# Cross-attention queries multiplied by blocks, and sums and loads moved to other steps, in a decoder with gated cross-attention

## The chip, the cores and the metric

The kernel runs on one core of a Trainium2 chip, in float32. The metric is device time in microseconds (us), the median of several runs. The engines are TensorE (PE, with its weight loads PEld), VectorE (DVE), ScalarE (ACT), GpSimd (POOL) and SyncE (SP), whose queue issues nearly all DMA transfers. Every engine works through its own instructions in the order of the program.

## The reference

Sixteen sequences of 128 tokens with 512 features go through a decoder layer (self-attention, cross-attention to an encoder context, MLP, each after a layer norm and added to the residual), and then through a gated cross-attention to the same context. Sixteen heads have 32 features each.

```python
ln_out = layernorm(hidden_states, ln1_s, ln1_b)
q, k, v = jnp.split(ln_out @ w_qkv + b_qkv, 3, axis=-1)
x = hidden_states + merge_heads(attention(split_heads(q), split_heads(k), split_heads(v), ltor_mask)) @ w_ao + b_ao
q = layernorm(x, ln2_s, ln2_b) @ w_q + b_q
k, v = jnp.split(encoder_states @ w_kv + b_kv, 2, axis=-1)
x = x + merge_heads(attention(split_heads(q), split_heads(k), split_heads(v), cross_mask)) @ w_co + b_co
x = x + gelu(layernorm(x, ln3_s, ln3_b) @ w1 + b1) @ w2 + b2
# gated: Q = x Wq', K and V from layernorm(context), a boolean mask
x = x + jnp.tanh(gate) * (out @ Wo.T)
```
`attention` multiplies the scores by the mask, subtracts 10000 (1 - mask), and takes a softmax over the keys.

## The kernel before

**Sections.** The 16 sequences are four groups of four batches. Each attention of a group is a section: A0 to A3 (self), B0 to B3 (cross), then the MLP over all groups, then D0 to D3 (gated). A section has 16 steps, four per batch. PE begins a batch in step 0, 4, 8 or 12 with its scores (into four "sc" PSUM banks), applies an older batch's probabilities to the values in steps 2, 6, 10, 14 (`mix`, the av matmuls), and makes its output projection (mo) two steps later. The work of a unit (four heads of a batch) moves down one step at a time: DVE scales the scores out of PSUM (`scale_unit`), POOL adds the mask term (`add_mask`); a step later DVE takes the minimum and ACT four exponentials with their sums (`exp_unit`); then DVE takes reciprocals and POOL normalizes (`norm_unit`); then DVE transposes within 32x32 squares and SP sends the unit to DRAM, from where pairs of units come back transposed (`receive_pair`).

**Beside a section.** While a section is attended, its steps also carry the projections of the next section (`jobs`) and the normalization and transposition of the tokens of the one after that (`prepare`): the queries, keys and values of B0 are made beside A3, those of B1 beside B0, of B2 beside B1, of B3 beside B2; beside B3 stand the start of the MLP and the first gated keys and values, beside D0 the projections of D1. `plan` collects lists of jobs with their steps, written out by hand. In each step the order is: receive, scores, what was put off by `afterwards` (DVE's first, then ACT's), the jobs, an older output projection, mix, prepare, transpose, normalize and exponentials, scale, mask (`attend`, lines 657 to 701).

**Blocks.** Most projections are done with seven quarter products instead of eight (`block_product`, lines 383 to 424): the operands are cut in 2x2 blocks, four sums of the weight's blocks (`left_blocks`) and four of the tokens' (`right_blocks`, in part in place) are made first, and products 1 to 7, of four matmuls 128x256 each, are added up. Products 1, 6 and 7 pile up in one PSUM bank ("mm0") and ACT copies it out after each, at once; 5 and 3 use "mm1" and 2 and 4 one of the two banks "pt", which the mix and the output projection use too; DVE adds these in the next step. Product 1 needs no sum; 6 needs the third weight sum and the second token sum, 7 the first and the third, 5 the second and the first, 3 the fourth weight sum, 4 the fourth token sum. `BLOCKS` (line 464) holds the steps of a self-attention section's three products, `CROSS_BLOCKS` (line 480) those of the cross keys and values. The cross queries are made in four chunks of four matmuls 128x512, in "mm0" and "mm1", copied out by ACT (`query_chunk`, line 921).

**Buffers.** Weights and weight sums lie in a pool of six buffers "w"; masks and some sums in two buffers "mask"; scores in seven "s"; parts received and gated tokens in three "pT". The token sums of a cross section's keys and values lie in the residual x of the group, which is put away in DRAM meanwhile (`keep_part`, `tokens_again`).

Of the kernel before, what the change touches and what calls it, by code (L numbers as in the profile page):

```python
# [16 lines left out]
P = 128  # L17
NB = 16
S = 128
Q = 32  # L20
# [32 lines left out]
def decoder_then_gated_cross_attention(ctx: ExitStack, tc: tile.TileContext, a: dict, out: bass.AP):  # L53
# [406 lines left out]
    def by_quarters(t):  # L460
# [17 lines left out]
    )  # L478

    CROSS_BLOCKS = (  # L480
        {6: (1,), 7: (6, 2), 9: (7, 5), 10: (4,), 11: (3,)},
        {11: (1,), 13: (6, 2), 14: (7, 5), 15: (4, 3)},
    )
    GATED_BLOCKS = (
# [156 lines left out]
    def attend(sections, ready, others, after=None):  # L641

        if not ready:
            sections[0].start(sections[1])
        at_start[0] = False
        units, batches = [], []  # L650
        projected = deque()

        def by_transfer(n):

            return min(n, (len(sections) * GB - 1) * GB) if ready else n

        def step(k, bt=None, jobs=(), ahead=None):

            m = k % GB
            pair = k - 5  # L660
            if pair % 2 and 0 <= pair < by_transfer(len(units)):
                receive_pair(*units[pair])
            if m == 0 and bt is not None:
                scores(bt)
            due()
            for job in jobs:
                job()
            if projected and (m == 0 or ready and bt is None):
                before = projected.popleft()
                if before.sec.deferred:  # L670
                    afterwards("act", lambda: before.sec.put_away(before))
                else:
                    out_project(before)
            done = k // GB - 2
            if ready and k == by_transfer(k) + 7:
                done = len(batches) - 1
                mix(batches[done])
                projected.append(batches[done])
            elif m == 2 and 0 <= done < len(batches) - ready:
                mix(batches[done])  # L680
                projected.append(batches[done])
            if ahead is not None:
                ahead.prepare(k % NS)
            if 0 <= k - 3 < len(units):
                (turn_unit if k - 3 < by_transfer(k) else turn_by_array)(*units[k - 3])
            def norm():
                if 0 <= k - 2 < len(units):
                    norm_unit(*units[k - 2])

            def exp():  # L690
                if 0 <= k - 1 < len(units):
                    least_unit(*units[k - 1])
                    exp_unit(*units[k - 1])


            for do in (exp, norm) if ready else (norm, exp):
                do()
            if bt is not None:
                for j in SCALED[m]:
                    scale_unit(bt, j)  # L700
                bt.sec.add_mask(by_head(bt.s[m]), bt.b)

        k = 0
        for i, sec in enumerate(sections):
            last = i + 1 == len(sections)
            jobs = others() if last else sections[i + 1].jobs()
            ahead = sections[i + 2] if i + 2 < len(sections) else after if i + 2 == len(sections) else None
            for b in range(GB):
                bt = Batch(sec, b)
                batches.append(bt)  # L710
                for m in range(GB):
                    units.append((bt, m))
                    step(k, bt, jobs.get(k % NS, ()), ahead)
                    k += 1
        while projected or k < len(units) + 2 * GB:
            step(k, jobs=jobs.get(k - len(units) + NS, ()))
            k += 1
# [14 lines left out]
    class SelfAttention(Section):  # L732
# [19 lines left out]
        def begin(self, following):  # L752
# [24 lines left out]
            for o in SelfAttention.weight_sums[0]:  # L777
                nc.gpsimd.tensor_tensor(*o)
            following.prepare(0)
            transposed_out(self.lnT, tp, "ln1_s", "ln1_b")  # L780

        def start(self, following):

            self.begin(following)
            _, todo = self.tiles()
            for o in todo:
                nc.vector.tensor_tensor(*o)
            key_sums, value_sums = self.weight_sums[1:]
            prepare = [lambda p=p: following.prepare(p) for p in (2, 4, 6, 9, 12, 13)], [0, 1, 2, 4, 6, 6]
            jobs = plan(  # L790
                *blocks_plan(self.products(), FIRST_BLOCKS), prepare,
                ([lambda o=o: nc.gpsimd.tensor_tensor(*o) for o in key_sums], [0, 1, 2, 3]),
                ([lambda o=o: nc.gpsimd.tensor_tensor(*o) for o in value_sums], [4, 5, 6, 6]),
                ([load_small, lambda: mask_terms(ms1, ma1)], [2, 5]),
                ([lambda b=b: load_batch(2, b) for b in range(2)], [3, 5]),
            )
            for p in range(max(jobs) + 1):
                due()
                for job in jobs[p]:
                    job()  # L800
            due()
# [18 lines left out]
        def jobs(self):  # L820
# [3 lines left out]
            if g > 1:  # L824
# [3 lines left out]
            return plan(  # L828
                *blocks_plan(first.products()[2:], FIRST_BLOCKS), (sums, [2, 3, 4, 5]),
                *blocks_plan(self.products(), SECOND_BLOCKS), *small_jobs(),  # L830
                ([lambda p=p: self.prepare(p) for p in (14, 15)], [0, 0]),
                ([lambda b=b: add_row(0, bo_row, b) for b in range(GB)], range(8, 12)),
                *gated_weight("k", act_tile("gw_k", "enc"), range(4, 12), range(9, 16, 2)),
            )
# [23 lines left out]

    def late_weights():

        return [lambda key=key, k=k: load_cross(key, k) for key in ("ck", "cv", "co") for k in range(KC)], range(12)

    class CrossAttention(Section):
        w_o = property(lambda self: w["co"])
# [32 lines left out]

        def jobs(self):
            g, n, lnT, encT = self.g, self.name, self.lnT, self.encT
            mask = work.tile([P, 2, GB, S], F32, tag="mask", name=f"mask_{g}", bufs=2)  # L900
# [4 lines left out]
            qkv_tiles(self)  # L905
            tokens_at = [x[g][:, b].rearrange("p (o t) -> p o t", t=HF) for b in range(3)]
            token_sides, sums = right_blocks(encT, tokens_at)
            if g == 0:
                self.begin()
            products = [  # L910
                block_product(halves(self.k), self.k_sides, token_sides, False, f"k_{n}", ("b_k", 0)),
                block_product(by_quarters(self.v), self.v_sides, token_sides, True, f"v_{n}"),
            ]
            return plan(
                ([lambda c=c: self.query_chunk(c) for c in range(KC)], [1, 2, 3, 5]),
                *blocks_plan(products, CROSS_BLOCKS), ([lambda: mask_terms(self.ms, self.ma)], [7]),
                ([lambda o=o: nc.gpsimd.tensor_tensor(*o) for o in sums], [0, 1, 2, 3]),
                *(self.weights_begin() if g == 0 else decoder[NG + g - 1].tokens_again([5, 9, 13])),
            )

        def query_chunk(self, c):
            project_chunk(self.q, w["cq"], self.lnT, c, f"q_{self.name}", "b_q", 0, ("mm0", "mm1")[c % 2])

        v_bias = "b_cv", 0

# [1 line left out]
            return [([lambda b=b: fetch_part(f"x_{self.name}", x[self.g], b) for b in order], at_)]  # L927

        def begin(self):
            t = wpool.tile([P, GB, 2, HF], F32, tag="w", name="sums_c")  # L930
            row = work.tile([P, 2, HF], F32, tag="row", name="sums_c_row", bufs=2)
            CrossAttention.sums_at = [t[:, n] for n in range(GB)] + [row, sums_c]
            CrossAttention.k_sides, CrossAttention.v_sides = [], []

        def weights_begin(self):

# [12 lines left out]
            def v_sum(n):  # L949
# [2 lines left out]
                todo["v"][n]()  # L952

            return (
                late_weights(), ([lambda n=n: k_sum(n) for n in range(4)], [4, 4, 5, 5]),
                ([lambda n=n: v_sum(n) for n in range(4)], [9, 10, 11, 12]),
            )

        def scale_mask(self, s, sc, b):
# [403 lines left out]
    class GatedAttention(Section):  # L1363
# [12 lines left out]
        def hidden_states(self, b, t=None):  # L1376
# [98 lines left out]
        def jobs(self):  # L1475
# [10 lines left out]
            by_dve, by_pool = (  # L1486
                lambda o, eng=eng: lambda: eng.tensor_tensor(*o) for eng in (nc.vector, nc.gpsimd)
            )
# [191 lines left out]
```

## Time and profile before

| | us |
|---|---|
| median of 3 runs (lowest, highest) | 1176.0 (1175.42, 1177.72) |
| profiled execution | 1175.37 |
| its span, first to last instruction | 1173.6 |
| A0 to A3, from scores to scores | 41.18, 103.13, 164.27, 225.41 to 288.33 |
| B0 to B3 begin at | 288.33, 350.06, 411.79, 474.79 |
| first gated scores | 950.89 |
| PE busy in the span | 1134.5 |

The profile's times are us from the span's start. A line of the order of time gives start, duration, engine, operation, the tile written and those read, the shape, how many were merged, and in brackets the idle time of the engine before it with what ended that. A line of a table by stretch gives, for every engine, its busy us and in brackets the number of instructions, then the granted clock of PE as a share of full speed, and DMA. All instructions have the same line number (L49, a helper's), so that one goes by tiles. The end of a section's last batches overlaps the next section's first.

### The profile page before, as it was taken

What the parts mean: (1) busy time and instruction counts of PE and PEld (TensorE: products, weight loads), DVE (VectorE), ACT (ScalarE), POOL (GpSimd) and SP (SyncE); (2) the same over time, 40 slices, a digit from 0 to 9 for tenths busy, and PEclk for the clock granted to TensorE, in tenths of its full rate; (3) what the DMA queues carried; (4) which work ended last, traced back from release to release, by engine and by line L of the source; (5) the groups of instructions that cost most, each with busy time, mean ns of one, the idle gap of its engine ahead of it and who ended that gap; (6) DMA issues with size and microseconds to landing.
All of it is one profiled execution on the core that took longest, in us unless ns stands there. A gap on an engine that the chain in (4) does not pass through costs nothing.

```text
span 1173.6 us, 21606 instructions
## 1 busy us (share of the span) xinstructions
PE 1134.5 (97%) x7202; PEld 864.2 (74%) x7202; DVE 766.9 (65%) x1513; ACT 608.4 (52%) x2129; POOL 698.0 (59%) x632
## 2 busy tenths in 40 slices
PE   6999999999999999998999999999999989999998
PEld 5877777657575747545788888888888767778775
DVE  7677878797878876865663633533432268878773
ACT  2467767666766766674221332232222238876763
POOL 6698878688868775684333423533441356554973
PEclk9999999999999999999999999999999999999999
DMA  6588968999888879998796686595467628888874
GB/s 217 150 219 226 234 191 216 252 235 252 212 230 203 243 208 242 253 285 260 249 291 225 195 263 200 193 310 207 153 204 249 188 61 230 227 233 238 243 208 160
DMA packets 325118, 259.75 MB, mean 221 GB/s; under 512 B 83528, under 2 KB 280336, under 8 KB 320144
## 3 DMA queue, kind: packets, MB, share of 16 engines
q1 hardware_dynamic: 324968, 258.38, 76.4%
q8 instruction: 57, 0.93, 0.3%
q14 instruction: 53, 0.43, 0.1%
q10 hardware_dynamic: 40, 0.01, 0.0%
HBM read 163.94 MB, written 94.37 MB: 220 GB/s over the span
## 4 chain that ended last, share of the span: by engine, by line
PE 49%; DMA 2%; DVE 2%; issue 1%; POOL 1%; ACT 1%; SPq 0%; DVEq 0%; POOLq 0%; ACTq 0%
PE o L49 16%; PE h L49 16%; PE mm_q_D L49 3%; PE mm_v_D L49 3%; PE mm_k_D L49 3%; PE mm_o_D L49 3%; PE sc_D L49 1%; PE av_D L49 1%; PE mo_D L49 1%; DMA away_B<-s_B 1%; PE mo_B L49 1%; SPq L49 0%; POOL x L49 0%; POOL s_B L49 0%; DVE s_D L49 0%
## 5 line engine op out<-in xcount | busy, mean ns | idle before, releaser
L49 DVE TENSOR_TENSOR h<-h,h 128x512 f32<-128x512 f32 x80 | 54.8, 686 | 112.8 <-PE h L49 112.5
L49 ACT ACTIVATE s_A<-s_A,mn_A 128x128 f32<-128x128 f32 x256 | 100.1, 395 | 50.9 <-issue 36.8
L49 ACT ACTIVATE s_B<-s_B,mn_B 128x128 f32<-128x128 f32 x256 | 100.1, 396 | 45.7 <-issue 31.8
L49 ACT ACTIVATE h<-h 128x512 f32<-128x512 f32 x64 | 40.4, 632 | 160.4 <-DVE h L49 160.4
L49 ACT ACTIVATE s_D<-s_D,mn_D 128x128 f32<-128x128 f32 x256 | 100.1, 393 | 33.1 <-issue 14.4
L49 POOL TENSOR_TENSOR s_D<-s_D,sum_D 128x512 f32<-128x512 f32 x64 | 66.5, 1039 | 73.0 <-DVE sum_D L49 59.9
L49 POOL TENSOR_TENSOR s_B<-s_B,sum_B 128x512 f32<-128x512 f32 x64 | 67.0, 1047 | 50.5 <-DVE sum_B L49 43.0
L49 POOL TENSOR_TENSOR s_A<-s_A,sum_A 128x512 f32<-128x512 f32 x64 | 66.6, 1041 | 36.7 <-DVE sum_A L49 34.6
L49 POOL TENSOR_TENSOR s_A<-s_A,ma 128x512 f32<-128x512 f32 x64 | 81.8, 1279 | 5.3 <-DVE s_A L49 3.7
L49 POOL TENSOR_TENSOR s_B<-s_B,mask 128x512 f32<-128x512 f32 x64 | 81.5, 1273 | 2.1 <-DVE s_B L49 0.4
L49 POOL TENSOR_TENSOR rstd_aD<-rstd_aD,mhalf 128x1 f32<-128x1 f32 x12 | 6.6, 549 | 114.7 <-DVE rstd_aD L49 101.2
L49 POOL TENSOR_TENSOR sh<-h 128x512 f32<-128x512 f32 x32 | 40.7, 1271 | 51.0 <-ACT h L49 43.0
L49 PE MATMUL mo_B<-w_co,mT_B 128*128 128x512 f32 x128 | 60.6, 617 | 3.0 <-ACT mT_B L49 3.0
L49 PE MATMUL h<-T_C,t 128*128 128x256 f32 x256 | 60.7, 380 | 1.6 <-DVE h L49 1.6
L49 PE MATMUL h<-T_C,w 128*128 128x256 f32 x256 | 61.0, 381 | 0.8 <-DVE h L49 0.8
L49 PE MATMUL h<-sx,t 128*128 128x256 f32 x256 | 60.6, 379 | 0.0
L49 PE MATMUL o<-t,h 128*128 128x256 f32 x256 | 60.5, 379 | 0.0
L49 PE MATMUL o<-t,sh 128*128 128x256 f32 x256 | 60.5, 379 | 0.0
L49 PE MATMUL o<-w,h 128*128 128x256 f32 x256 | 60.5, 379 | 0.0
L49 PE MATMUL mo_A<-w_ao,mT_A 128*128 128x512 f32 x128 | 59.1, 604 | 0.0
L49 PE MATMUL mm_q_B<-T_B,w_cq 128*128 128x512 f32 x128 | 57.3, 595 | 0.0
L49 PEld LDWEIGHTS h<-T_C,t 128*128 128x128 f32 x256 | 48.5, 190 | 9.3 <-DVE h L49 2.4
(324 smaller groups left out, 2997.3 us busy)
## 6 DMA issues: line engine op xcount, KB each, us to landing
t<-kept SPq DMA_DIRECT2D x24, 1024.0 KB, 8.3
away_A<-s_A SPq DMA_DIRECT2D x64, 256.0 KB, 3.5
pT_A<-away_A SPq DMA_DIRECT2D x128, 128.0 KB, 2.9
away_B<-s_B SPq DMA_DIRECT2D x64, 256.0 KB, 5.6
pT_B<-away_B SPq DMA_DIRECT2D x128, 128.0 KB, 4.0
away_D<-s_D SPq DMA_DIRECT2D x60, 256.0 KB, 3.4
pT_D<-away_D SPq DMA_DIRECT2D x120, 128.0 KB, 2.9
w<-in_L_xattn_w_dram SPq DMA_DIRECT2D x24, 512.0 KB, 5.2
```

Of the source, the lines that this page charges most:

```text
L49: return lambda *args, **kw: self.tc.keep_in_program_order(call(*args, **kw))
```

## The change

Cross queries go by seven quarter products with the plan `BLOCKS`, as in self-attention. Their four weight sums are made once, by DVE in steps 0, 1, 1 and 2 of A3, into a new "w" buffer (sums_cq); their four token sums by POOL in steps 0, 0, 1, 2 beside every section before a cross section, into a "mask" buffer and a quarter of sums_cq. The token sums of keys and values move from steps 0 to 3 to steps 4 to 7; the sums of the value weight from 9 to 12 to 9, 9, 10, 10. The mask of a cross section is loaded in step 13 and its terms are made in step 15, instead of before step 0 and in step 7. The cross output weight is loaded beside B0 (steps 7, 8, 8, 9) instead of beside A3 (steps 8 to 11).

At the start of the program three of A1's normalizations go by ACT with a scale and an offset (`rest_by_act`) instead of by DVE, its tokens come back a step later, and all four chunks are copied in step 0 of A0. Beside D0, the sums of the gated key weight go from DVE (steps 1, 1, 2, 2) to POOL (1 to 4), those of the value weight stay on POOL, in steps 6 to 9 instead of 4 to 7; the transposes of the last group's x by DVE move from steps 0 to 3 to steps 6, 8, 10, 12, into "s" buffers, with ACT's additions after them.

```diff
@@ attend
         if not ready:
             sections[0].start(sections[1])
-        at_start[0] = False
@@ SelfAttention.begin
             following.prepare(0)
+            at_start[0] = False
             transposed_out(self.lnT, tp, "ln1_s", "ln1_b")
@@ SelfAttention.start
-            prepare = [lambda p=p: following.prepare(p) for p in (2, 4, 6, 9, 12, 13)], [0, 1, 2, 4, 6, 6]
+            prepare = [lambda p=p: following.prepare(p) for p in (2, 4, 6, 9)], [0, 1, 2, 5]
@@ SelfAttention.jobs
-                ([lambda p=p: self.prepare(p) for p in (14, 15)], [0, 0]),
+                ([lambda p=p: self.prepare(p) for p in range(12, 16)], [0] * 4),
@@ late_weights
-        return [lambda key=key, k=k: load_cross(key, k) for key in ("ck", "cv", "co") for k in range(KC)], range(12)
+        return [lambda key=key, k=k: load_cross(key, k) for key in ("ck", "cv") for k in range(KC)], range(8)
+    output_weight = [lambda k=k: load_cross("co", k) for k in range(KC)]
@@ CrossAttention.jobs
+            free = work.tile([P, 2, 2, HF], F32, tag="mask", name=f"sums_T{g}", bufs=2)
...
+            q_sides, q_sums = right_blocks(lnT, [free[:, 0], free[:, 1], self.sums_at[6]])
             products = [
+                block_product(halves(self.q), self.q_sides, q_sides, False, f"q_{n}", ("b_q", 0)),
                 block_product(halves(self.k), self.k_sides, token_sides, False, f"k_{n}", ("b_k", 0)),
                 block_product(by_quarters(self.v), self.v_sides, token_sides, True, f"v_{n}"),
             ]
             return plan(
-                ([lambda c=c: self.query_chunk(c) for c in range(KC)], [1, 2, 3, 5]),
-                *blocks_plan(products, CROSS_BLOCKS), ([lambda: mask_terms(self.ms, self.ma)], [7]),
-                ([lambda o=o: nc.gpsimd.tensor_tensor(*o) for o in sums], [0, 1, 2, 3]),
+                *blocks_plan(products, BLOCKS),
+                ([self.load_masks, lambda: mask_terms(self.ms, self.ma)], [13, 15]),
+                ([lambda o=o: nc.gpsimd.tensor_tensor(*o) for o in q_sums], [0, 0, 1, 2]),
+                ([lambda o=o: nc.gpsimd.tensor_tensor(*o) for o in sums], [4, 5, 6, 7]),
                 *(self.weights_begin() if g == 0 else decoder[NG + g - 1].tokens_again([5, 9, 13])),
+                *(((output_weight, [7, 8, 8, 9]),) if g == 1 else ()),
             )
@@ CrossAttention.begin
-            t = wpool.tile([P, GB, 2, HF], F32, tag="w", name="sums_c")
+            t, u = (wpool.tile([P, GB, 2, HF], F32, tag="w", name=f"sums_{n}") for n in ("c", "cq"))
...
-            CrossAttention.sums_at = [t[:, n] for n in range(GB)] + [row, sums_c]
+            CrossAttention.sums_at = [t[:, n] for n in range(GB)] + [row, sums_c, u[:, 3]]
...
+            CrossAttention.q_sides, todo = left_blocks(w["cq"], [u[:, n] for n in range(3)])
+            CrossAttention.q_sums = [lambda o=o: nc.vector.tensor_tensor(*o) for o in todo]
@@ CrossAttention.weights_begin
-                late_weights(), ([lambda n=n: k_sum(n) for n in range(4)], [4, 4, 5, 5]),
-                ([lambda n=n: v_sum(n) for n in range(4)], [9, 10, 11, 12]),
+                late_weights(), (self.q_sums, [0, 1, 1, 2]), ([lambda n=n: k_sum(n) for n in range(4)], [4, 4, 5, 5]),
+                ([lambda n=n: v_sum(n) for n in range(4)], [9, 9, 10, 10]),
@@ GatedAttention.hidden_states, prepare
-            if t is None:
-                t = work.tile([P, NQ, KC, Q], F32, tag="pT", name=f"x_{self.name}_{b}", bufs=3)
+            t = work.tile([P, NQ, KC, Q], F32, tag=tag, name=f"x_{self.name}_{b}", bufs=3 if tag == "pT" else 7)
...
-            if g == 2 and p < GB:
-                gates[3].hidden_states(p)
-            elif g == 2 and 2 * GB <= p < 3 * GB:
-                gates[3].add_void(p - 2 * GB)
+            if g == 2 and p in (6, 8, 10, 12):
+                gates[3].hidden_states(p // 2 - 3, "s")
+            if g == 2 and p in (7, 9, 11, 13):
+                gates[3].add_void((p - 7) // 2)
@@ GatedAttention.jobs
-                    ([by_dve(o) for o in self.sums[1]], [1, 1, 2, 2]),
-                    ([by_pool(o) for o in self.sums[2]], [4, 5, 6, 7]),
+                    ([by_pool(o) for o in self.sums[1]], [1, 2, 3, 4]), ([by_pool(o) for o in self.sums[2]], [6, 7, 8, 9]),
```

More of the change, by code (lines that the diff above doesn't have):

```diff
@@ L478, in decoder_then_gated_cross_attention @@
     )
[L480 to L483, printed above, removed]
     GATED_BLOCKS = (
@@ L899, in jobs, with load_masks @@
             g, n, lnT, encT = self.g, self.name, self.lnT, self.encT
+            free = work.tile([P, 2, 2, HF], F32, tag="mask", name=f"sums_T{g}", bufs=2)
+            qkv_tiles(self)
+            tokens_at = [x[g][:, b].rearrange("p (o t) -> p o t", t=HF) for b in range(3)]
+            token_sides, sums = right_blocks(encT, tokens_at)
+            if g == 0:
+                self.begin()
+            q_sides, q_sums = right_blocks(lnT, [free[:, 0], free[:, 1], self.sums_at[6]])
+            products = [
+                block_product(halves(self.q), self.q_sides, q_sides, False, f"q_{n}", ("b_q", 0)),
+                block_product(halves(self.k), self.k_sides, token_sides, False, f"k_{n}", ("b_k", 0)),
+                block_product(by_quarters(self.v), self.v_sides, token_sides, True, f"v_{n}"),
+            ]
+            return plan(
+                *blocks_plan(products, BLOCKS),
+                ([self.load_masks, lambda: mask_terms(self.ms, self.ma)], [13, 15]),
+                ([lambda o=o: nc.gpsimd.tensor_tensor(*o) for o in q_sums], [0, 0, 1, 2]),
+                ([lambda o=o: nc.gpsimd.tensor_tensor(*o) for o in sums], [4, 5, 6, 7]),
+                *(self.weights_begin() if g == 0 else decoder[NG + g - 1].tokens_again([5, 9, 13])),
+                *(((output_weight, [7, 8, 8, 9]),) if g == 1 else ()),
+            )
+        def load_masks(self):
+            g = self.g
             mask = work.tile([P, 2, GB, S], F32, tag="mask", name=f"mask_{g}", bufs=2)
@@ L904, in jobs @@
             )
[L905 to L914, printed above, removed]
-                ([lambda c=c: self.query_chunk(c) for c in range(KC)], [1, 2, 3, 5]),
-                *blocks_plan(products, CROSS_BLOCKS), ([lambda: mask_terms(self.ms, self.ma)], [7]),
-                ([lambda o=o: nc.gpsimd.tensor_tensor(*o) for o in sums], [0, 1, 2, 3]),
[L918 to L922, printed above, removed]
         v_bias = "b_cv", 0
@@ L1374, in normalized, with hidden_states @@
             return lambda: normalize_and_send(raw, t[:, 1], self.a_away, f"a{n}", b)
-        def hidden_states(self, b, t=None):
-            if t is None:
-                t = work.tile([P, NQ, KC, Q], F32, tag="pT", name=f"x_{self.name}_{b}", bufs=3)
+        def hidden_states(self, b, tag="pT"):
+            t = work.tile([P, NQ, KC, Q], F32, tag=tag, name=f"x_{self.name}_{b}", bufs=3 if tag == "pT" else 7)
             nc.vector.transpose(by_chunk(t), squares(x[self.g][:, b, :]))
@@ L1485, in jobs @@
             ]
-            by_dve, by_pool = (
-                lambda o, eng=eng: lambda: eng.tensor_tensor(*o) for eng in (nc.vector, nc.gpsimd)
-            )
+            by_pool = lambda o: lambda: nc.gpsimd.tensor_tensor(*o)
             more = ()
```

## The prediction

> **What bounds the kernel now.** I read the totals by engine first, then the busy time of each engine in one stretch per section (A1, A2, A3, B0, B1, B2), then the order of time of each engine in A2 and A3.
>
> ```profile
> PE 1134.5 (97%) x7202; PEld 864.2 (74%) x7202; DVE 766.9 (65%) x1513; ACT 608.4 (52%) x2129; POOL 698.0 (59%) x632
> ```
> TensorE (PE) is busy 97% of the span: work taken from it counts, unless another engine then makes it wait.
>
> ```profile
> core 0: us, PE busy (x) PEld busy (x) DVE busy (x) ACT busy (x) POOL busy (x), PEclk, DMA share, GB/s
> ...
> 164.27:225.41 61.14, 60.34 (x458) 44.44 (x457) 49.55 (x104) 42.35 (x168) 48.51 (x45) 1.00 0.85 224
> 225.41:288.33 62.92, 61.76 (x433) 39.87 (x432) 54.15 (x106) 41.51 (x164) 53.52 (x49) 1.00 0.95 246
> 288.33:350.06 61.73, 61.72 (x433) 39.96 (x432) 49.04 (x102) 42.96 (x169) 48.93 (x45) 1.00 0.83 221
> 350.06:411.79 61.73, 61.72 (x433) 39.96 (x432) 49.05 (x102) 42.33 (x165) 48.21 (x45) 1.00 0.84 218
> 411.79:474.79 63.00, 61.86 (x434) 39.88 (x433) 48.08 (x102) 41.73 (x165) 42.83 (x40) 1.00 0.86 233
> ```
> These are sections A2, A3, B0, B1 and B2. In each PE is nearly full, but in A3 VectorE (DVE) has 54.15 us of work and GpSimd (POOL) 53.52 us in 62.92 us. A2 runs beside it the projections of A3 by blocks, all three: it is the model of what the last four become.
>
> **The queries by blocks.** A chunk is eight PE records of 3.43 us, four make 13.7 us. A quarter product takes 1.73 us back to back, seven make 12.1 us. That is 1.6 us less PE work per section, 6.4 us in four. The A2 plan has one wait of its own, 0.78 us in step 14 (a value product waits for DVE's add of a key product in the same bank), while A3 and B2 now have one of 1.15 us each that the new steps remove (key products 1 and 6 move two steps apart). So I take the difference of sections as they stand: all four at 61.14 us instead of 62.92, 61.73, 61.73 and 63.00: 1.8 + 0.6 + 0.6 + 1.9 = **4.8 us less**, if DVE and POOL keep up. What they get per section: three or four more adds on DVE (0.69 us each, 0.6 us in a row) and four more token sums on POOL (1.27 us each, 5.1 us).
>
> **Section A3, where they don't keep up.** In steps 0 to 2 of A3 DVE also gets the four sums of w_cq, and keeps its four of w_ck in steps 4 and 5. What such a sum costs beside a busy POOL:
>
> ```profile
> start us, us, engine line op out<-in xcount [idle before <-releaser]
> ...
> 240.63 1.05 POOL L49 TENSOR_TENSOR s_A<-s_A,sum_A 128x512 f32<-128x512 f32 x1
> 240.72 1.51 DVE L49 TENSOR_TENSOR sums_c<-w_ck 128x512 f32<-128x512 f32 x1
> 241.63 1.73 POOL L49 TENSOR_TENSOR s_A<-s_A,ma 128x512 f32<-128x512 f32 x1
> 242.26 1.64 DVE L49 TENSOR_TENSOR w_ck<-w_ck 128x512 f32<-128x512 f32 x1
> 243.32 1.72 POOL L49 TENSOR_TENSOR x<-x,bco_row 128x512 f32<-128x512 f32 x1
> ...
> 247.40 1.26 DVE L49 TENSOR_TENSOR sums_c<-w_ck 128x512 f32<-128x512 f32 x1
> 248.70 0.69 DVE L49 TENSOR_TENSOR sums_c<-w_ck,sums_c 128x512 f32<-128x512 f32 x1
> ```
> The sum of two SBUF operands takes 0.69 us with POOL idle; beside POOL it ends 0.6 us after POOL's running instruction does, and POOL's next one is 0.45 us longer. The mean of the four is 1.28 us. POOL has no idle time to speak of in steps 0 to 4 of A2, so I price the new four at 4 x 1.28 = 5.1 us (ends: 4 x 0.6 = 2.4 and 4 x 1.64 = 6.6). DVE ended step 5 of A3 at 251.75, 26.3 us into the section. Added before that point: 5.1 us of sums and 1.2 us for two query adds; taken off: the 1.2 us that DVE waited for an output projection. That is 31.4 us; then a transpose (0.63) and the add of query product 4 (0.65) of step 6: 32.7 us.
>
> Who waits for that add? Query product 4 is in a "pt" bank since step 5, key product 2 is in the other since step 6, and the mix (av) of step 6 needs one of these two. In A2 it starts without a wait at 26.3 us (190.54), DVE having made the add by 188.19:
>
> ```profile
> 187.54 0.65 DVE L49 TENSOR_TENSOR q_A<-q_A,mm_q_A 128x512 f32<-128x512 f32 x1
> ```
> ```profile
> 188.72 1.89 PE L49 MATMUL mm_k_A<-T_A,w_sk 128*128 128x256 f32 x8
> 190.54 1.08 PE L49 MATMUL av_A<-pT_A,v_A 128*32 128x128 f32 x32
> 191.55 1.99 PE L49 MATMUL mm_k_A<-sums_A,sums 128*128 128x256 f32 x8
> ```
> The old chunks used other banks, so nothing of the kind stood there. So PE waits 32.7 - 26.3 = 6.4 us (with the low price of a sum 3.7, with the high one 7.9). Such a wait costs more than its length: after the 3.38 us wait at 962.92 the granted clock fell (0.69 mean over 967 to 972, one stretch of 3.4 us at half clock); half of that is 1.7 us. Behind it, POOL has sums in steps 4 to 7 and two each in 9 and 10 (it had four, one per step, in 9 to 12), so that value product 6 in step 11 comes some 1.6 us late. A3: 61.1 + 6.4 + 1.7 + 1.6 = 70.8, **7.9 us more** than 62.92 (2 to 10).
>
> **B0 and B1.** The key and value token sums move to steps 4 to 7. In A2 POOL ended its mask of step 7 at 195.44, 31.2 us in. Four sums of 1.27 us, less the 2.1 us that POOL idled in these steps: 34.2. The mask terms move to step 15, ahead of the reciprocal that POOL's normalization waits for: their two instructions take 0.43 to 1.53 us, 1.96 in all, and DVE's idle time there is behind them; I take 1.5 us (0 to 2). That makes 35.7. Then DVE's minimum (0.65), ACT's four exponentials (1.66) and the copy of key product 7 (0.84) follow in order, and value product 1 of step 10 shares its bank: 39.0 instead of 37.3 in A2, 1.7 us of wait, and some 0.3 at the mix of step 6. Each: 61.14 + 2.0 = 63.1, **1.4 us more** than before (-0.6 to +3). B2 has no rows to add on POOL (42.83 us): it takes the gain, **1.9 us less**.
>
> **Loads.** The load of w_co is issued in steps 7 to 9 of B0. Six weight buffers hold then w_ao, sums_c, sums_cq, w_cq, w_ck and w_cv; so its first part waits in SP's queue for the last output projection with w_ao in step 8, and behind it wait a probability transfer (3.5 us to landing) and four receives, which the mix of step 10 needs. PE's work between is some 8 us; I take 0.5 us (0 to 3). The mask is loaded in step 13 and used in 15; it landed in 3.8 to 5.5 us, two steps are about 7 us: nothing, or 1 us a section without that cover.
>
> **Start.** Three normalizations go from DVE (1.48, 1.48, 0.82 us) to ACT, idle there, and leave 0.2 us each. PE's only wait in that stretch, 1.48 us at 27.45, is for DVE's add at 28.09, behind two of them. I take **1.3 us less** (-1.5 to +1: the receive and ACT's four copies come a step later, and ACT had 1.87 us idle at 42.4).
>
> **First gated section.**
> ```profile
> 956.56 1.76 DVE L49 TENSOR_TENSOR gsums<-w_gk 128x512 f32<-128x512 f32 x1
> 958.35 1.64 DVE L49 TENSOR_TENSOR w_gk<-w_gk 128x512 f32<-128x512 f32 x1
> ```
> ```profile
> 966.29 1.69 PE L49 MATMUL sc_D<-k_D__7892,q_D 32*128 32x128 f32 x26 [3.38 <-DVE s_D L49]
> 967.91 3.05 PE L49 MATMUL mm_q_D<-x,w_gq 128*128 128x256 f32 x8
> ```
> DVE's four key sums (4.8 us) and four transposes of x (2.8 us) make it late, the scores wait 3.38 us, and the next matmuls run at half clock: key product 1 starts at 970.80 where back-to-back work would be at 964.7, 6.1 us. Both loads leave DVE's first steps. What is late next is POOL: sums one per step in 1 to 4 with 1.27 us for the key ones, so the normalization of step 3 ends near 967.6, the transpose of step 4 follows, ACT's exponentials end near 970.7, and only then does ACT copy key product 1; product 6 starts near 971.5 instead of 974.26. **2.8 us less** (6.1 to 0). The transposes in steps 6 to 12 take an s buffer (seven, of which I count six in use): nothing, or 0.7 us each.
>
> [...]
>
> **Sum**, against the profiled execution (1175.37 us: span 1173.6 and 1.8 around it; 0.6 below the median of 1176.0): A3 +7.9, B0 and B1 +2.8, B2 -1.9, w_co +0.5, start -1.3, gated -2.8: +5.2, 1180.6; on the median 1181.
>
> **Rivals.** (1) *All hidden*: DVE and POOL keep up, each section 61.14: -4.8 - 1.3 - 2.8 = -8.9, **1167**. For it: A2 does it with the same blocks. Against: 54 us of DVE work in A3, plus 8. (2) *A3's wait halves*: with sums at 0.6 us and no loss of clock A3 gains nothing or loses 2, B0 and B1 stay even: 2 + 0 - 1.9 - 1.3 - 2.8 = -4, **1172**. For it: POOL's order may leave gaps. (3) *The gated start gives all 6.1 us* and A3 loses 6: 6.0 + 1.5 - 1.9 - 1.3 - 6.1 = -1.8, hardly a change: **1174**. Against: POOL's row of sums. (4) *Slower still*: GpSimd is the bound of B0 and B1 too, from the point where its lag reaches value product 1 (2 us late at step 7), plus w_co in SP's queue: A3 +10, B0 and B1 +3 each, w_co +3, the rest -6: **1189**.
>
> **Chances.** Forecast 0.43, (1) 0.12, (2) 0.15, (3) 0.17, (4) 0.13. 0.2%, 2.4 us, is about what a measurement of this kernel can tell from no change: faster 0.27, same 0.17, slower 0.56. The range of 8 in 10 goes from 1168, leaving out most of (1), to 1188, leaving out half of (4).
>
> **What would show it.** In the profile after: sc to sc of A3 near 70 us with a PE wait at an av in its first half, ended by a DVE q_B add, and the clock below 1 after it; DVE sums of w_cq above 1 us; B0 and B1 near 63, B2 near 61; no wait of the scores near 962. The forecast is wrong if A3 stays under 65 us, or if that av starts without a wait.

## The result, and the profile after

The changed kernel takes **1185.57 us** (median of 4 runs, 1185.26 to 1185.81) against 1176.15 (4 runs, 1175.42 to 1177.72): ratio 1.0076, 95% interval 1.0060 to 1.0092. It is slower, inside the forecast range and 4.6 us above the forecast time. The profiled execution has a span of 1183.5 us, 9.9 more than before.

The totals of the page after:

```profile
PE 1133.5 (96%) x7298; PEld 885.3 (75%) x7298; DVE 773.4 (65%) x1529; ACT 608.3 (51%) x2140; POOL 722.6 (61%) x652
```
PE is busy 1.0 us less and POOL 24.6 us more, for the quarter products bring sums. As the span is 9.9 us longer, PE stands idle 10.9 us more. The table by stretch, for A2, A3, B0, B1, B2 of the changed kernel (us with the number of instructions, then clock and DMA):

```profile
core 0: us, PE busy (x) PEld busy (x) DVE busy (x) ACT busy (x) POOL busy (x), PEclk, DMA share, GB/s
162.44:223.58 61.14, 60.35 (x458) 44.47 (x457) 49.58 (x104) 42.13 (x169) 48.47 (x45) 1.00 0.87 221
223.58:293.59 70.01, 62.90 (x457) 45.91 (x456) 61.16 (x114) 41.60 (x166) 59.09 (x52) 0.98 0.81 208
293.59:361.33 67.74, 62.08 (x458) 45.58 (x457) 50.82 (x106) 42.60 (x172) 53.71 (x49) 0.97 0.84 216
361.33:422.46 61.13, 60.34 (x458) 44.46 (x457) 51.30 (x106) 41.31 (x164) 52.04 (x49) 1.00 0.85 219
422.46:486.60 64.14, 61.96 (x457) 45.48 (x456) 49.52 (x106) 42.98 (x172) 49.28 (x45) 0.97 0.87 234
```
Read the first number of each row against the same section before. B1 is what the forecast's "all hidden" rival had for all four, 61.1 us. A3, B0 and B2 are longer, and in each PE busy is also higher than in A2 and the clock below 1: a wait, and slow matmuls after it. The whole account, profiled execution against profiled execution:

| part | change, us | forecast |
|---|---|---|
| start, to the first scores | -1.8 | -1.3 |
| A3 | +7.1 | +7.9 |
| B0 | +6.0 | +1.4, and 0.5 for w_co |
| B1 | -0.6 | +1.4 |
| B2 | +1.1 | -1.9 |
| B3 and the MLP | -1.6 | 0 |
| first gated section | -1.1 | -2.8 |
| the rest | +0.8 | 0 |

**A3** has the forecast wait at the forecast place. PE's order of time in the changed kernel:

```profile
250.17 1.89 PE L49 MATMUL mm_k_B<-T_e,w_ck 128*128 128x256 f32 x8
256.63 1.80 PE L49 MATMUL av_A<-pT_A,v_A 128*32 128x128 f32 x32 [4.56 <-DVE q_B L49]
258.36 3.11 PE L49 MATMUL mm_k_B<-x,sums_c 128*128 128x256 f32 x8
```
DVE's add of query product 4 ended at 256.57; the product after the mix takes 3.11 us where 1.89 to 1.99 is usual, at a granted clock of 0.51 from 257.3 to 260.7.

**B0** has a wait that the forecast did not have. SP's issues in the changed kernel:

```profile
320.66 0.38 SPq L49 DMA_DIRECT2D away_B<-s_B  x1
328.06 0.35 SPq L49 DMA_DIRECT2D w_co<-in_L_xattn_w_co_dram  x1
...
332.17 0.38 SPq L49 DMA_DIRECT2D turned_B<-ln_B  x1
...
334.82 0.50 SPq L49 DMA_DIRECT2D w_co<-in_L_xattn_w_co_dram  x1
335.64 0.83 SPq L49 DMA_DIRECT2D back_B<-turned_B  x2
...
341.20 1.57 SPq L49 DMA_DIRECT2D back_B<-turned_B  x2
```
The first part of w_co stands 7 us at the head of the queue until w_ao's buffer is free; B1's normalized tokens are sent (turned_B) and brought back (back_B) behind it. What waits for them, all engines in order of time:

```profile
348.35 0.81 ACT L49 ACTIVATE T_B<-back_B,vcols 128x512 f32<-128x512 f32 x1 [7.76 <-DMA back_B<-turned_B]
...
350.73 0.18 DVE L49 RECIPROCAL sum_B<-sum_B 128x4 f32<-128x4 f32 x1 [4.80 <-ACT s_B L49]
...
352.59 0.68 DVE L49 TENSOR_TENSOR k_B<-mm_k_B,k_B 128x512 f32<-128x512 f32 x1
...
353.32 1.22 PE L49 MATMUL mm_v_B<-w_cv,x 128*128 128x256 f32 x2 [5.29 <-DVE k_B L49]
```
Read it downwards: ACT's copy of T_B waits for the transfer; the exponentials are queued behind that copy (their minimum was ready at 342.42, the first began at 349.06); DVE's reciprocal waits for them; DVE's add of key product 3 is queued behind the reciprocal (PE had ended the product at 348.03, the add began at 352.59); and value product 5, in the same bank, waits for the add. A queue and three engines in a row, and each waits for the one before.

**B2** has the end of the same chain, behind the gated tokens (back_a), for which ACT had waited 4.72 us before the change too:

```profile
473.41 0.81 ACT L49 ACTIVATE T_a<-back_a,vcols 128x512 f32<-128x512 f32 x1 [4.94 <-DMA back_a<-turned_D]
...
478.39 1.83 PE L49 MATMUL mm_v_B<-w_cv,x 128*128 128x256 f32 x5 [2.17 <-DVE k_B L49]
```

**The gated start** shows both ends of its step: the scores no longer wait, and key product 6 does.

```profile
972.07 1.17 PE L49 MATMUL sc_D<-k_D__7995,q_D 32*128 32x128 f32 x32
...
981.11 3.53 PE L49 MATMUL mm_k_D<-gsums_a,gsums 128*128 128x256 f32 x8 [2.49 <-ACT k_D L49]
```
The forecast had 971.5 for product 6; everything here is 10.2 us later, so 981.7.

### The profile page after: what moved, and what is told of

It reads as the page before. It is cut to its first block, busy times and chain, and to the rows that moved or that the text cites. A ratio compares the mean times of both kernels' runs of the same rounds, so it can differ in the third digit from the quotient of the medians.

```text
span 1183.5 us, 21843 instructions
## 1 busy us (share of the span) xinstructions
PE 1133.5 (96%) x7298; PEld 885.3 (75%) x7298; DVE 773.4 (65%) x1529; ACT 608.3 (51%) x2140; POOL 722.6 (61%) x652
## 4 chain that ended last, share of the span: by engine, by line
PE 52%; DVE 2%; POOL 2%; issue 1%; ACT 1%; DMA 1%; SPq 0%; DVEq 0%; POOLq 0%; ACTq 0%
PE o L49 16%; PE h L49 16%; PE mm_k_D L49 4%; PE mm_v_D L49 4%; PE mm_o_D L49 3%; PE mm_q_D L49 3%; PE mo_B L49 2%; PE av_D L49 1%; PE mo_D L49 1%; PE sc_D L49 1%; PE mm_v_B L49 1%; POOL x L49 1%; PE av_B L49 0%; DVE s_D L49 0%; DMA away_B<-s_B 0%
## 5 line engine op out<-in xcount | busy, mean ns | idle before, releaser
L49 PE MATMUL h<-sx,t 128*128 128x256 f32 x256 | 60.6, 380 | 0.0
L49 DVE STREAM_TRANSPOSE s_D<-s_D 128x512 f32<-128x512 f32 x60 | 42.3, 705 | 21.2 <-POOL s_D L49 21.0
```

Source lines behind the costliest of these rows:

```text
L49: return lambda *args, **kw: self.tc.keep_in_program_order(call(*args, **kw))
```

## The experiments

The forecast's theory of A3 is DVE's lag at one bank; the theory formed after the result puts B0's 6.0 us down to the place of w_co's load. Rivals stand with each run. Section lengths are from each run's own profile; where only one execution was made, times are not compared, sections are.

**1. w_co later.** The edit, in the changed kernel:
```diff
-                *(((output_weight, [7, 8, 8, 9]),) if g == 1 else ()),
+                *(((output_weight, [9, 9, 10, 10]),) if g == 1 else ()),
```


> The changed kernel with the load of w_co in steps 9 and 10 of B0 (two parts each) instead of 7, 8, 8, 9. Theory: B0's 6.0 us come from this load, whose first part waits in SP's queue and holds up the transfers behind it, until ACT copies T_B late and value product 5 waits in step 14. Then that wait of 5.29 us falls below 1 us, B0 goes from 67.74 to 61.1 us, and the time from 1185.6 to about 1179. Rival: DVE and POOL lag in B0 by themselves (more sums and adds). Then the wait in step 14 stays above 3 us, B0 above 65, and the time above 1184. A3 stays at 70.0 by both.

Measured: 1182.09 us (5 runs; 1.0056, 1.0029 to 1.0083); A3 70.04, B0 65.97. The wait in step 14 fell to 0.79 as the theory has it, but B0's number missed: the two late parts were issued at 339.0, landed after their use, and a new wait came ahead of the first output projection.

```profile
345.28 2.78 PE L49 MATMUL mo_B<-w_co,mT_B 128*128 128x512 f32 x4 [2.45 <-DMA w_co<-in_L_xattn_w_co_dram]
```

**2. w_co between the two.** All four parts in step 9: `[9] * 4`.

> The changed kernel with all four parts of the load of w_co in step 9 of B0: after the last projection with w_ao has let its buffer go, but 9 us ahead of the two late parts of e1_co_later (issued at 339.0 there, used at 340.8). Theory: all of B0's 6.0 us are the place of this load in SP's queue. Then there is neither a wait of 5.29 us in step 14 nor one of 2.45 us for w_co, and B0 is 61.1 to 62 us (67.74 in the changed kernel, 65.97 in e1_co_later). Rival: B0 has no place for this load without a cost; then another transfer behind it comes late (back_B, or the probabilities) and B0 stays above 64. A3 70.0 by both.

Measured, in one execution: B0 **61.95** (A3 70.35).

```profile
294.59:356.54 61.95, 60.43 (x457) 44.36 (x456) 51.21 (x106) 41.84 (x169) 52.85 (x49) 1.00 0.92 234
```
```profile
344.99 0.81 ACT L49 ACTIVATE T_B<-back_B,vcols 128x512 f32<-128x512 f32 x1 [3.39 <-DMA back_B<-turned_B]
```
There is no wait for w_co; ACT's wait for the tokens is 3.39 us instead of 7.76, and that in step 14 is 1.16. Here 5.8 of B0's 6.0 us go with the load's step, but the step alone does not settle it. Runs 5, 6, 7 and 11 have the load in step 9 too; there ACT waits 4.0 to 4.7 us and B0 has 65.19, 64.36, 62.87 and 65.70 us. The steps of run 1 gave 63.01 in run 3 and 68.35 in run 9. What the ten kernels with this load beside B0 have in common is ACT's idle time ahead of its first copy of the next section's tokens, 2.8 to 7.8 us; in B0 of the four kernels without it, and in B1 of all fourteen, it is 0.0 to 1.8 us. So the load beside B0 goes with the late tokens; that one step is the right one for it is not shown.

**3. Query product 4 a step earlier** (with the edit of 1):
```diff
-                *blocks_plan(products, BLOCKS),
+                *blocks_plan(products, ({1: (1, 2), 2: (6,), 3: (7, 5), 4: (4,), 6: (3,)}, *BLOCKS[1:])),
```


> The kernel of e1_co_later with cross query product 4 moved from step 5 to step 4, so that the mix of step 6 finds a bank that DVE has freed earlier. Theory: A3's 7.1 us are the wait for that one bank. Then the wait of 4.56 us at the mix goes, nothing of its size takes its place, and A3 falls from 70.0 to 64 or 65 us. Rival: the lag of DVE itself costs, whatever bank shows it. Then the wait moves: the scores of step 8, or a product before them, wait for DVE's work of step 6 some 3 us or more, and A3 stays at 68 to 70. B0 to B3 as in e1_co_later.

Measured: the rival; A3, at 71.22, is above even its 68 to 70. PE of this kernel:

```profile
250.54 1.99 PE L49 MATMUL mm_k_B<-T_e,w_ck 128*128 128x256 f32 x8 [0.58 <-DVE q_B L49]
...
259.44 1.26 PE L49 MATMUL sc_A<-k_A,q_A 32*128 32x128 f32 x26 [2.96 <-DVE s_A L49]
261.85 2.07 PE L49 MATMUL mo_A<-w_ao,mT_A 128*128 128x512 f32 x2 [1.16 <-ACT mT_A L49]
```
The mix no longer waits; the scores of step 8 wait for DVE's scaling, and the projection after them. The bank only showed the lag.

**4. B0's queries by chunks** (with the edit of 1): `query_chunk` restored for g = 0, the four sums of w_cq by POOL in steps 12 to 15 of A3.

> The kernel of e1_co_later with the queries of B0 by chunks again, which A3 computes, and the four sums of w_cq by POOL in steps 12 to 15 of A3 instead of by DVE in steps 0 to 2. Theory: A3's loss is DVE's sums and query adds in its first steps. Then A3 goes from 70.0 to 61.5 to 63 us (62.92 before the change), with no PE wait above 1.2 us. Rival: other parts of the change are behind A3's loss (mask terms in step 15, POOL's sums in steps 4 to 7, the value sums of w_cv by twos in steps 9 and 10). Then A3 stays above 66. B0 to B3 as in e1_co_later.

Measured: A3 64.87, between the two: no wait for DVE, one of 1.59 us at value product 6 for POOL's sum (sums_c_row), and PE's larger work for the chunks. Against run 1 A3 is 5.2 us shorter, so the blocks of B0's queries, with their sums and adds, are most of A3's loss of 7.1; of the 2.0 us that stay, the wait for POOL is 1.6.

**5. The sums of w_cq earlier.** On top of 2, w_cq loaded in steps 8 to 11 of A2 and summed by POOL in steps 14 and 15 there:
```diff
+            if g == 0 and p >= 14:
+                for o in self.q_todo[2 * p - 28 : 2 * p - 26]:
+                    nc.gpsimd.tensor_tensor(*o)
...
```


> The kernel of e6_co_step9 with w_cq loaded in steps 8 to 11 of A2 (was 12 to 15) and its four sums made by POOL in steps 14 and 15 of A2 (were made by DVE in steps 0 to 2 of A3). Queries stay by blocks in all four sections. Theory: A3 loses because these sums stand at the head of DVE's work there. Then the wait of 4.56 us at the mix falls below 1.5 us and A3 to 62 to 64 us; time about 1173 with B0 at 61.5. Rival: DVE is full in A3 without them (query adds, four sums of w_ck, the mask terms), so a wait of 2 us or more stays, and A3 is 66 or above, time 1177 or above.

Measured: 1178.66 us (10 runs; 1.0019, 1.0004 to 1.0034), A3 **70.61** with the mix waiting 4.62 us: the four sums, 4.4 us, had left DVE, and it was no earlier. B0 has 65.19 us and not the 61.5 that was expected (see run 2). What DVE waited for in steps 0 to 4 of A3, and its first sum of w_ck, beside POOL's order of time:

```profile
DVE s_A L49 <- POOL s_A L49: 1.6, 2, 0.8
DVE mn_A L49 <- POOL s_A L49: 1.2, 3, 0.5
...
DVE off_B L49 <- POOL rstd_B L49: 0.8, 2, 0.5
```
```profile
242.67 3.38 DVE L49 TENSOR_TENSOR sums_c<-w_ck 128x512 f32<-128x512 f32 x1
```
```profile
241.77 1.28 POOL L49 TENSOR_TENSOR s_A<-s_A,ma 128x512 f32<-128x512 f32 x1
243.00 1.28 POOL L49 TENSOR_TENSOR x<-x,bco_row 128x512 f32<-128x512 f32 x1
244.22 1.28 POOL L49 TENSOR_TENSOR x<-T_e 128x512 f32<-128x512 f32 x1
```
From its first sum of w_cq at 217.2 to 245.5 POOL is busy 28.06 of 28.30 us, so that it comes late to everything in the first steps of A3; DVE waited 3.6 us for it and spent 2.1 us more in that one sum (1.31 in the changed kernel). What was taken from DVE came back as waits for POOL: the pair is full, not DVE alone.

**6. No sums of w_cq at all** (on top of 2; this kernel leaves them out, its queries are not those of the reference).

> The kernel of e6_co_step9 without the four sums of w_cq (left out: the query products of the cross attention take plain blocks of w_cq in their place). All else stands, the token sums on POOL in steps 0 to 2 of A3 and the query adds on DVE too. Theory: DVE's 4.4 us of sums at the head of A3 are the larger part of the loss, as the forecast had it. Then the wait at the mix falls from 4.57 to below 1 us and A3 from 70.35 to 62 to 64 us. Rival, from e7_early_cq, where these sums left A3 and its wait stayed at 4.62 us: DVE and POOL wait for each other through the softmax units, and what counts is the sum of what both get. Then DVE has gaps that POOL ends in steps 0 to 4, a wait of 2 to 4 us stays, and A3 is 65.5 to 69.

Measured: the rival. A3 67.68, the mix still waits:

```profile
254.13 1.71 PE L49 MATMUL av_A<-pT_A,v_A 128*32 128x128 f32 x26 [3.52 <-DVE q_B L49]
```
DVE waited 1.4 us for POOL and ACT in steps 3 and 4, and its four sums of w_ck took 6.3 us in steps 4 and 5, ahead of the add. Those sums stood there before the change too, and nobody waited for them. In A2, which has the same blocks and no weight sums, the add came 23.9 us after the section's start; here 29.8. So of A3's +9.2 over A2 (experiment 2), 2.7 go with the sums of w_cq. The 5.9 us by which the add is still later are close to the length of these old sums. That it is they, which the new plan no longer covers, is argued and not shown: no run took them away.

**7. Key product 3 a step earlier** (on top of 5), in the plan that all block sections share:
```diff
-        {5: (1,), 6: (2,), 7: (6,), 9: (7, 5), 10: (4,), 13: (3,)},
+        {5: (1,), 6: (2,), 7: (6,), 9: (7, 5), 10: (4,), 12: (3,)},
```


> The kernel of e7_early_cq with key product 3 in step 12 instead of 13 in the plan that self- and cross attention share, so that value product 5 of step 14, in the same bank, finds DVE's add made. Theory: the wait of 0.78 us in step 14 that A1 to B2 have, and its longer forms in B0 (5.29) and B2 (2.17), come from that pair alone: they go, A2 and B1 fall from 61.1 to 60.4, B2 from 64.1 to 60.4, and the time is 6 to 8 us below e7_early_cq. Rival: what is late is DVE, and only the place where PE meets it moves: a wait at the output projection of step 12, at the mix of step 14 or at the scores of the next step 0 takes its place, and sections stay within 0.3 us.

Measured: 1182.71 us (10 runs; 1.0058, 1.0041 to 1.0074): slower than 5. A1 and A2 fell to 60.6 and B2 to 60.61 as the theory has it, but A3 rose to 72.22 and B1 to 62.78 (61.13), with new waits of 0.23, 0.59 and 0.96 us in B1; B0 fell from 65.19 to 62.87. Half of each theory: the pair of products makes the wait of step 14, and where DVE is near its limit the wait moves. The two profiled executions differ by 0.3 us only (1180.13 and 1180.39), so the sections do not explain the 4 us between the medians.

**8. The start alone**, and **9. the gated part undone.** Run 8 is the kernel before with the start's edit; run 9 is run 1 with the gated edit taken back.

> The kernel before with the change of the start alone (the three normalizations of the second batch group after the start code on ACT, two prepares one step later). Theory: the first scores start at 39.3 us instead of 41.2, and the rest is that of the kernel before, so 1174.3 us. Rival: the 1.8 us are a difference between executions (first scores came at 39.3, 39.5, 39.8, 39.7 and 41.3 us in the changed kernel and its four variants): then they start at 40.5 or later, and the time is 1175 or more.

> The kernel of e1_co_later with the gated part undone: key sums on DVE in steps 1 and 2, x transposed at the start of the first gated section. Theory: that part gave 1.8 us, the wait of the scores (3.38 us in the kernel before) less the new wait of product 6 (2.49 us, with a slower clock behind it). Then the scores wait about 3.4 us again, the wait at product 6 goes, and the first gated section is 1.5 to 2.1 us longer than in e1_co_later. Rival: the part gave nothing, and the difference of the two traces is where the half-speed stretches of the clock fall. Then the section is within 0.5 us of that in e1_co_later.

Measured: in 8 the first scores start at 39.61, all sections to B1 are those of before within 0.1 us, 1172.24 us (one run, where the kernel before ran from 1172.13 to 1179.53). In 9 the scores wait 3.38 us again and the section has 52.87 us, 2.4 more than in run 1: the theory's wait, a little above its size. Run 9 has the start's edit too and its first scores came at 41.34; its clock was 0.51 from 23.0 to 26.5 us, which no other run has in the start. In the other executions the start's gain is 0.9 to 1.8 us.

**10. The start, and of the gated part the transposes only**, on the kernel before: key sums stay on DVE.

> The kernel before with the change of the start and, of the gated part, only the earlier transposes of x (from the s buffers); the key sums stay on DVE and the value sums in steps 4 to 7. Theory: the transposes (2.8 us of DVE work) are what made the scores wait 3.38 us, and the new wait of 2.49 us at key product 6 comes from the key sums on POOL. Then the scores wait 0.3 to 0.8 us, no half-speed stretch follows, the first gated section falls from 52.87 to 48 or 49 us, and the time is 1168 to 1170. Rival: the key sums on DVE are enough to hold the scores (4.8 us, lengthened beside POOL). Then a wait above 1.5 us stays and the section is above 50.5 us.

Measured: **1170.22 us** (10 runs), 0.9948 of before, 0.9930 to 0.9967: faster. The first gated section is 49.18 us, 3.7 less than before:

```profile
961.44 1.12 PE L49 MATMUL sc_D<-k_D__7898,q_D 32*128 32x128 f32 x26 [1.30 <-DVE s_D L49]
```
and product 6 follows without a wait (967.96). The wait of 1.30 is longer than expected, its cure is the expected one. In the profiles the start gives 0.9 us and this section 3.7; the rest of the distance between the medians lies in sections that the edit does not touch, and no run explains it. Moving the key sums to POOL as well costs 0.7 to 2.6 us of this (49.83 to 51.79 in the runs with both).

**11. Blocks for the queries of B1 to B3 only** (on top of 10): A3 as in the kernel before, w_cq summed by DVE in steps 13 to 15 of A3, w_co in step 9 of B0.

> The queries by blocks in B1, B2 and B3 only: B0's are computed in A3 by chunks as in the kernel before, with its steps for mask, token sums and key and value products; the four sums of w_cq by DVE in steps 13 to 15 of A3, w_co loaded in step 9 of B0, and start and gated section as in e10_start_and_turns. Theory: the gain of the blocks is there wherever DVE and POOL have room: A3 63, B0 62, B1 61.1, B2 61 to 62.8, some 2 us less than e10_start_and_turns. Rival: the adds and sums cost as much in B0 to B2 as the products save; then the time is within 1 us of e10_start_and_turns or above it.

Measured: the rival's time, 1172.96 us (10 runs; 0.9961, 0.9943 to 0.9979). A3 62.86 and B1 61.13 as expected; B0 65.70 and B2 64.92, with value product 5 waiting 2.43 and 2.95 us for DVE's add of key product 3. The rival's reason, that adds and sums cost what the products save, is not shown: in both sections ACT had waited for tokens before that (4.66 us for back_B, 5.72 for back_a), and B1, with the same adds and sums, gained its 0.6 us.

**12. Blocks for the queries of B3 only** (on top of 10), with key product 3 in step 12 there and in A1 and A2; the sums of w_cq by DVE in steps 3, 5, 12 and 15 of B1.

> The kernel of e10_start_and_turns with two more edits: key product 3 in step 12 in the self-attention plan that runs in A1 and A2, and the queries by blocks for B3 alone, which B2 computes; there POOL has no rows to add. The four sums of w_cq are made by DVE in steps 3, 5, 12 and 15 of B1, and w_co is loaded in A3 as in the kernel before. Theory: the blocks pay in the one section where DVE and POOL have room. A1 and A2 60.6 us each (61.1), B1 stays at 61.7, B2 60.6 to 61.1 (64.3 in e10_start_and_turns, 63.0 in the kernel before), all else as in e10_start_and_turns: some 4 us less than its 1170.2, 1166 to 1168. Rival: the sums in B1 bring its value products late (B1 63 or more), or B2's wait in step 14 comes back in another place; then the time is 1169 or above, no better than e10_start_and_turns.

Measured: 1169.59 us (6 runs; 0.9937, 0.9924 to 0.9950), no different from 10 (the intervals overlap). The sections did about what was expected: A1 60.60 and A2 60.59, B1 62.42 (for 61.7), B2 60.59 against 64.32. B3 began 4.5 us earlier than in 10, and the first gated scores came 0.8 us later. B3's first three batches, in 12 and then in 10:

```profile
470.68:486.92 16.24, 16.24 (x97) 7.71 (x96) 15.37 (x38) 8.90 (x37) 10.69 (x11) 1.00 0.74 196
486.92:501.62 14.70, 13.28 (x90) 6.35 (x89) 12.68 (x28) 12.53 (x52) 11.81 (x12) 1.00 0.98 266
501.62:515.71 14.09, 13.21 (x90) 6.35 (x89) 7.33 (x14) 6.43 (x30) 8.82 (x9) 1.00 1.04 292
```
```profile
475.19:491.44 16.25, 16.25 (x98) 7.72 (x97) 15.24 (x39) 9.95 (x38) 10.66 (x12) 1.00 0.83 224
491.44:504.24 12.80, 12.80 (x89) 6.18 (x88) 9.06 (x19) 8.49 (x37) 8.54 (x8) 1.00 1.04 289
504.24:517.05 12.81, 12.81 (x89) 6.19 (x88) 8.59 (x17) 8.17 (x38) 11.18 (x11) 1.00 1.06 305
```
The second and third batch are 1.9 and 1.3 us longer, and PE's waits there are for probabilities on their way back (2.9 us for pT_B at av up to 530, none of that kind in 10 up to 531). In both kernels DVE is full in the first batch, so that units leave no earlier, and the DMA engines are full from the second on (a share of 0.98 to 1.06); which of the two makes the probabilities late, no run settles. There is another part: from 528.0 to 534.8 us the clock was 0.51 and 0.50 in 12 and full in 10, worth up to 3.4 of the 5.3 us. Nor does the early arrival alone explain it: run 8 came to B3 at 473.75, 1.0 us ahead of the kernel before, and from there to the gated scores took 473.10 us for 476.10.

## Why the prediction was right, and where its sizes were off

The time came out 4.6 us above the forecast, and part of its closeness is luck: the terms miss by -2.0 to +4.1 us, 14.5 us taken without sign, and their sum is 4.7. The fourth rival's 1189 was nearer by 1.2 us; of its conditions w_co in SP's queue held, a GpSimd bound in B0 and B1 did not. Of the signs named ahead, those of A3 and of the gated scores came (though only two of the four sums of w_cq took over 1 us), and those of B0, B1 and B2 did not. The mechanism of the largest term is what held.

- **A3, +7.9, measured +7.1**: the sum's largest term held with its place (the mix of step 6), its releaser (the add of query product 4) and nearly its size. Forecast: DVE ends step 5 31.4 us into A3, the add 32.7, PE waits 6.4; measured 31.7, 33.0 and 4.6, because PE itself came there 28.5 us into A3 and not 26.3 (waits of 0.68 and 0.82 us ahead of it among them). The four sums took 0.68, 0.68, 1.65 and 1.42 us, 4.4 for a forecast of 5.1. The half-speed stretch came, 3.4 us at 0.51, which is the 1.7 us of the forecast. Value product 6 was 0.2 late instead of 1.6. What the forecast had too simple: it charged the w_cq sums with 5.1 us of the wait, and runs 5 and 6 show that without them on DVE 3.5 to 4.6 us of wait stay. In run 5 POOL is full; in run 6 it is most likely DVE's old w_ck sums.
- **w_co, +0.5 with an upper end of 3, measured 5.8 by run 2**: the mis-sized term. (B0 is 6.6 us longer than B1 of the same kernel, which has no such load; before the change both had 61.73. The load in step 9 gave back 2.0 to 5.8 us of it.) The step "its first part waits in SP's queue, and behind it wait a probability transfer and four receives, which the mix of step 10 needs" was right on the queue and wrong on who is late: the mix was not, the tokens' way out and back was. The forecast asked what the queue holds for the present section, and not what `prepare` sends through it for the next.
- **B0 and B1, +1.4 each**: value product 1 never waited for ACT's copy. POOL's later sums and the mask terms in step 15 (0.88 and 1.48 us) found cover; B1 is at 61.1 us. (The forecast's own terms add up to 38.9, not 39.0.)
- **B2, -1.9, measured +1.1**: step 14 again. DVE's add of key product 3 was late, after ACT had waited 4.94 us for back_a (4.72 before), and value product 5 waited 2.17 us; over the kernels with this plan that wait is 0.8 to 3.0 us and B2 61.1 to 64.9, so that the forecast's 61.1 was about met in runs 5 and 9 (61.25 and 61.14), and this +1.1 is one draw among several (B2 with the old plan is 63.0 to 64.3 in the kernel before and in runs 8 and 10). The forecast saw the wait of 0.78 in A2 and took it for fixed; it is a place where PE meets whatever lag DVE has.
- **Start, -1.3, measured -1.8**: right; in run 9, with its half-speed stretch in the start, it was nothing.
- **Gated, -2.8, measured -1.1**: right in both halves (product 6 came at 981.1 for a forecast of 981.7). The rest lies in the clock: its 2.49 us wait was followed by a product of 3.53 us, and 2.4 us are gained between runs 1 and 9.
- **Loads of the mask, 0**: right.

## What to carry to other kernels

Fewer matmuls by block sums moved work to the engines that make the sums (POOL 24.6 us more, DVE 6.5, for 1.0 less on PE): add up what each of them has to do up to each step, both together if they hand units to each other, and count old work whose cover the new plan takes away. A load that must wait for a buffer belongs behind the step that frees the buffer, and ahead of its use by its landing time (6.6 us for w_co in run 1); here the first part of w_co stood 7 us at the head of SP's queue, and what was issued behind it was late, also what is for the next section (ACT waited 7.76 us for its tokens). Ask too what the load displaces where it does not wait: in step 9 it still went with tokens that came late. Here the better kernel was the small part of the change that took work off a late engine (run 10), and 4.5 us won ahead of a stage with full DVE and full DMA engines were lost in it (run 12).

## What the runs showed of the hardware

- **Half speed followed idle time within one window of 3.41 us, not the length of a wait.** The last wait of note is 2.10 us in the changed kernel and 2.11 before; after it the granted clock was 0.51 for 3.4 us in the one and 1.00 in the other, and the product behind it took 3.64 us in the one and 1.99 in the other. The changed kernel has six such half-speed stretches ahead of its last 1.3 us, the kernel before two. Their starts lie whole multiples of 3.413 us apart: 28, 65, 83, 212 and 259 after the first, and 128 in the kernel before. Counted in windows of that grid in these two profiles, from where their clock records begin (14.9 us into the span after, 17.8 before), all nine windows at full speed with 2.0 us or more of idle PE time were followed by half speed, and none of the six with 1.2 to 1.9. Of the wait of 2.10 us 2.05 lie in one window, of that of 2.11 us 1.9.
- **A DVE sum of two SBUF operands beside POOL ended behind three POOL instructions.** In run 5 it began at 242.67 and ended at 246.05, 0.55 us after the third of three POOL instructions in a row, which took 1.28 us each (the mean of a mask addition by POOL, of the same shape, is 1.27 in the changed kernel). The next such sum, at 246.09 with POOL idle, took 0.69 us. In the rows of the kernel before that the forecast was worked out from, a sum ended 0.55 us after one POOL instruction. Why it ended behind one there and behind three here, no run shows.
